# Layer 0's edge types turned in memory, and the softmax stretches of layers 1 and 2 shifted by half a stretch

## The chip, the cores and the metric

The program runs on one core of one Trainium2 chip. Its time is the device time of one execution in microseconds (us). The engines are TensorE (PE), which multiplies matrices, with its weight loads shown as PEld; VectorE (DVE); ScalarE (ACT); GpSimd (POOL), which issues the indirect gathers here; and SyncE (SP), which issues most of the plain transfers. 16 DMA engines carry the transfers.

## The reference

Four graph layers run one after the other over the same graph: 3,125 nodes with 256 features and 50,000 edges, each with a source and a destination. After each layer x becomes layernorm(x + layer(x)). The parts that the change touches, cut to what matters:

```
# layer 0: 16 edge types
e = edge_emb[edge_type]
att_in = concat(x[src], x[dst], e, task)
delta = tanh(gelu(att_in @ att_W1 + b1) @ att_W2 + b2)
w = 1 + edge_scale * delta
agg = segment_sum(messages(x[src], e) * w, dst)
# layer 1: 4 heads, 8 relations; layer 2: 8 heads
score = per edge and head
m = segment_max(score, dst);  ex = exp(score - m[dst])
alpha = ex / segment_sum(ex, dst)[dst]
out = segment_sum(alpha * value[src], dst)
```

Layer 3 is a relational layer with block-diagonal weights; the change does not touch it.

## The kernel before

At the start the edges are sorted by destination and put into 416 *slot tiles* of up to 128 edges. Each slot tile belongs to one of the 25 node tiles of 128 nodes. Four slot tiles make a *group* (104 groups, G = 4) and 16 make a *stretch* (26 stretches, S = 16). The node features stay in SBUF; tables that edges gather from lie in memory.

**Startup.** `bucket` sorts and `segments` (L360) writes, for each slot tile, five rows of marks for the segmented softmax (`seg`): which slots hold an edge and where a node begins and ends. It does so in four chunks of up to 128 slot tiles: matmuls pick each tile's edges (L376, L380), DVE makes the marks (L383 to L400), small matmuls collect the values at tile edges (`astart`, `aend`, `anew`; L402), and an SP transfer stores the chunk. `rows` holds what one tile hands to the next within a stretch.

**Layer 0** walks the groups as a pipeline of three steps, in one loop. `gathered` issues four gathers on POOL (helper at L509) and makes two one-hots of each slot tile on DVE: the place of the edge's destination in its node tile (L928, `places[:, 0]`), and the edge's type (L931), which is copied three times side by side, once for each of three bf16 terms of the type table, into `places[:, 1]` (L934). PE turns both, eight 128x128 transposes a group (L939), and ACT copies the result out of PSUM into `oht` (L943). After every second group SP stores the place one-hots and the turned ones for layers 1 and 2 (`oh_d`, `oht_d`, 256 KB each). `attended` sums the attention's first layer in PSUM (`pre`): the gathered rows with an identity (L956), the destination's part through the turned place one-hot (L961), the type's part through the turned type one-hot and the table `ec` (L964). ACT applies gelu (L965) and DVE multiplies by the second weight and sums along the row (`hg`, L967). `summed` makes the edge weight on ACT (L972, L973), scales the place one-hot by it (`ohw`, L976), and PE sums the messages by destination (`pa`, L979, three PSUM buffers), which DVE adds to `acc` (L981). The two `places` buffers are made once and their unused columns are zeroed at the start (a memset on POOL at L918, another on DVE).

**Layers 1 and 2** share `edge_softmax` (L714). For each stretch it scores the four groups, while it weighs and sums the four groups of the stretch before, and then runs `softmax` (L607), which takes the maximum by destination with scans along the slots of the stretch, hands the state to the next stretch, and gives `ex`. The scores come from a product with the turned one-hots (L1237 in layer 1, L1398 in layer 2; DVE at L1242, L1243 and L1403 to L1405). `weigh` (L682) multiplies the gathered values by `ex` (L697 on DVE, L701 on ACT), sums by destination on PE (L706), and adds to `acc` on DVE (L711). The one-hots come back from memory for eight slot tiles at a time on SP's queue (`onehots_back`, L541), the marks once a stretch (L615, L619). At the beginning of the third stretch of layer 2 (t0 == 2 * S) deferred work, kept in `self.later`, is run.

The program is written in a tile framework: a scheduler fixes the order of the instructions on each engine, and an engine's queue is in order. A buffer of a pool is released as a whole, once everything that reads it is done.

Of the kernel before, what the change touches and what calls it, by code (L numbers as in the profile page):

```python
# [9 lines left out]
F32 = mybir.dt.float32  # L10
BF = mybir.dt.bfloat16
# [7 lines left out]
P = 128  # L19
# [14 lines left out]
class Net:  # L34
# [178 lines left out]
    def bucket(self, src, dst, type16, type8, weight, relations):  # L213
# [12 lines left out]
        self.s_w = c.tile([P, TT], F32, name="s_w")  # L226
        NS = TT // S

# [6 lines left out]

        self.seg = self.dram.tile([TT, 5, P], F32, name="seg")

        self.rows = self.dram.tile([NS, 2, S], F32, name="rows")
        self.astart, self.aend, self.anew = (c.tile([1, TT], F32, name=n) for n in ("astart", "aend", "anew"))
        self.tnode = c.tile([1, TT], I32, name="tnode")  # L240

        with tc.tile_pool(name="bk", bufs=1, side="right") as b:
# [40 lines left out]
            with tc.tile_pool(name="bkw", bufs=1, side="right") as w, tc.tile_pool(name="bkp", bufs=1, space=PSUM) as ps:  # L283
# [73 lines left out]

                self.segments(w, bd, nxt, prv, bdf, sel, kd)

    def segments(self, w, bd, nxt, prv, bdf, sel, kd):  # L360

        tc, nc, TT = self.tc, self.nc, self.TT
        C = bd.shape[1]
        flag = w.tile([P, 2, C, P], F32, name="flag")
# [4 lines left out]
        with tc.tile_pool(name="sgp", bufs=1, space=PSUM) as ps, tc.tile_pool(name="sg", bufs=2, side="right") as v:  # L369
            rows = ps.tile([1, 3, 512], F32, name="rows")  # L370
            for m0 in range(0, TT, P):
# [7 lines left out]
                for k in range(C):  # L379
# [4 lines left out]
                                        op0=ALU.add, op1=ALU.add)  # L384
                nc.vector.tensor_scalar(low[:M], low[:M], float(P), None, op0=ALU.mult)
                sg = v.tile([P, 5, P], F32, name="sg")
                dl = v.tile([P, P], F32, name="dl")
# [13 lines left out]
                for n, col in enumerate((sg[:M, 3, P - 1:P], sg[:M, 4, 0:1], edge[:M])):  # L401
                    nc.tensor.matmul(rows[:, n, m0:m0 + M], col, self.ident[:M, :M], start=True, stop=True)  # L402
                nc.sync.dma_start(self.seg[m0:m0 + M], sg[:M])
            for n, row in enumerate((self.astart, self.aend, self.anew)):
                nc.vector.tensor_copy(row, rows[:, n, :TT])
            rrow = w.tile([1, TT // S, 2, S], F32, name="rrow")
            nc.vector.memset(rrow, NEG)
# [199 lines left out]
    def softmax(self, w, sm, ps, hand, acc, sc, H, F, t0):  # L607
# [4 lines left out]
        nc = self.nc  # L612
        R = H * S
        sg = w.tile([R, 5, P], F32, name="sgm")
        nc.sync.dma_start(sg, bass.AP(tensor=self.seg.tensor, offset=self.seg.offset + t0 * 5 * P,  # L615
                                      ap=[[0, H], [5 * P, S], [1, 5 * P]]))
        s_of = t0 // S
        rr = w.tile([1, 2, H, S], F32, name="rr")
# [33 lines left out]
        nc.vector.scalar_tensor_tensor(hand[(s_of + 1) % 2][:, 0, :, 0], o[:, 0, :, S - 1],  # L652
                                       self.astart[:, t0 + S - 1:t0 + S], outf[:, :, S - 1],
                                       op0=ALU.add, op1=ALU.max)
        if s_of:
            nc.vector.scalar_tensor_tensor(ends[:, 1], o[:, 1, :, 0], self.aend[:, t0:t0 + 1], outb[:, :, 0],
                                           op0=ALU.add, op1=ALU.max)
# [9 lines left out]
        if s_of:  # L667
            dif = sm.tile([1, H], F32, name="dif")
            nc.vector.scalar_tensor_tensor(dif, ends[:, 1], self.anew[:, t0:t0 + 1], o[:, 0, :, 0],
                                           op0=ALU.add, op1=ALU.max)  # L670
            nc.vector.tensor_sub(dif, o[:, 0, :, 0], dif)
            at = sm.tile([1, P], F32, name="at")
            nc.vector.tensor_scalar(at, self.iota[0:1, :], self.s_dl[0:1, t0:t0 + 1], None, op0=ALU.is_equal)
            nc.tensor.matmul(mis[:, 400:400 + H], at, dif, start=True, stop=True)
            fac = sm.tile([P, H], F32, name="fac")
            nc.scalar.activation(fac, mis[:, 400:400 + H], AF.Exp)
            node = self.node_of(nc.vector, t0)
            a3 = acc[:, ds(node * (H * F), H * F)].rearrange("p (h f) -> p h f", h=H)
            self.used(nc.vector, nc.vector.tensor_mul(a3, a3, fac[:, :, None].to_broadcast([P, H, F])))
        yield ex  # L680

    def weigh(self, w, ps, acc, ohb, ex, value, H, t0, on_act):  # L682
# [7 lines left out]
        r = w.tile([P, G, H, F], F32, name="r")  # L690
        s0 = t0 % S
        oh = w.tile([P, G, P], F32, name="oh")
# [21 lines left out]
    def edge_softmax(self, w, sm, ps, hand, acc, H, F, score, on_act):  # L714
# [7 lines left out]
        nc = self.nc  # L722
        before, ex = [], None
        for t0 in range(0, self.TT + S, S):
            last = t0 == self.TT
            if t0 == 2 * S:
                with self.tc.issue_after(self.uses[nc.vector.engine][-1]):
# [3 lines left out]
            if not last:  # L731
                sc = sm.tile([P, H, S], F32, name="sc")
            for n in range(S // G):
                if not last:
                    held.append(score(t0 + n * G, sc[:, :, n * G:(n + 1) * G]))
                if before and (last or n < S // G - 1):
                    value, oh = before[n]
                    done(self.weigh(w, ps, acc, oh, ex, value, H, t0 - S + n * G, on_act))
            if last:
                break  # L740
            rest = iter(())
            if before:
                value, oh = before[-1]
# [10 lines left out]
    def layer0(self, task, edge_emb, msg_W, msg_b, att_W1, att_b1, att_W2, att_b2, edge_scale,  # L754
# [9 lines left out]
        with ExitStack() as layer:  # L764
# [22 lines left out]
            lng = vec(ln_g, D, "lng")  # L787
            lnb = vec(ln_b, D, "lnb")
            ec = wp.tile([P, D], BF, name="ec")
            nc.vector.memset(ec, 0.0)  # L790
            one = wp.tile([P, 1], F32, name="one1")
            nc.vector.memset(one, 1.0)
# [3 lines left out]
            with tc.tile_pool(name="n0", bufs=2) as w, tc.tile_pool(name="m0", bufs=1) as wm, \  # L796
# [20 lines left out]
                ul = film_loads(ua_W1, ua_b1, ua_W2, ua_b2, "ua")  # L817
                E3 = 3 * ET
                emb = wm.tile([E3, D], F32, name="emb")
# [61 lines left out]
                nc.vector.tensor_add(fst[:, 1:2], fst[:, 0:1], fst[:, 2:3])  # L881
                nc.vector.tensor_scalar(fst[:, 1:2], fst[:, 1:2], -1.0, 1.0, op0=ALU.mult, op1=ALU.add)
                nc.vector.tensor_scalar(ecs, part[:, 0, :], fst[:, 0:1], None, op0=ALU.mult)
                for n, o in ((1, ecs), (2, ec[:E3])):
# [26 lines left out]
            with tc.tile_pool(name="e0g", bufs=5) as gp, tc.tile_pool(name="e0", bufs=3) as w, \  # L911
# [3 lines left out]

                places = [hp.tile([P, 2, 2, G, P], BF, name="places%d" % n) for n in range(2)]
                for n, oh in enumerate(places):
                    (nc.vector if n % 2 else nc.gpsimd).memset(oh[:, 1], 0.0)  # L918
                ohts = [None]

                def gathered(t0):
                    gb = gp.tile([P, G, ET + XA], F32, name="gb")
                    for j in range(G):
                        self.gather(gb[:, j, ET:], table, self.s_src, t0 + j)
                    g = t0 // G % 2
                    both = places[t0 // (2 * G) % len(places)]
                    oh = both[:, :, g]
                    nc.vector.tensor_tensor(  # L928
                        oh[:, 0], self.iota[:, None, :].to_broadcast([P, G, P]),
                        self.s_dl[:, t0:t0 + G][:, :, None].to_broadcast([P, G, P]), op=ALU.is_equal)  # L930
                    nc.vector.tensor_tensor(  # L931
                        gb[:, :, 0:ET], self.iota[:, None, :ET].to_broadcast([P, G, ET]),
                        self.s_ty[:, t0:t0 + G][:, :, None].to_broadcast([P, G, ET]), op=ALU.is_equal)
                    nc.vector.tensor_copy(oh[:, 1, :, 0:3 * ET].rearrange("p j (n e) -> p j n e", n=3),  # L934
                                          gb[:, :, None, 0:ET].to_broadcast([P, G, 3, ET]))
                    pt = ps.tile([P, 2, G, P], BF, name="ohp")
                    for n in range(2):
                        for j in range(G):
                            nc.tensor.transpose(pt[:, n, j, :], oh[:, n, j, :], self.idb)  # L939
                    if not g:  # L940
                        ohts[0] = hp.tile([P, 2, 2, G, P], BF, name="oht", bufs=2)
                    oht = ohts[0][:, :, g]
                    nc.scalar.copy(oht, pt)  # L943
                    if g:
                        for to, of in ((self.oh_d, both), (self.oht_d, ohts[0])):
                            nc.sync.dma_start(to[t0 // (2 * G)], of[:, 0].rearrange("p g j v -> p (g j v)"))
                    return t0, gb, oh, oht

                def attended(t0, gb, oh, oht):
                    hg = w.tile([P, G, D], F32, name="hg", bufs=2)  # L950
                    dl = w.tile([P, G], F32, name="dl")
                    for j0 in range(0, G, 2):
# [4 lines left out]
                        for j in (j0, j0 + 1):  # L957
                            q = pre[:, j - j0, :]
                            node = self.node_of(nc.tensor, t0 + j)
                            for n in range(3):  # L960
                                last = nc.tensor.matmul(q, oht[:, 0, j, :], xbr[:, ds(node * (3 * D) + n * D, D)],  # L961
                                                        start=False, stop=False)
                            self.used(nc.tensor, last)
                            nc.tensor.matmul(q, oht[:, 1, j, :], ec, start=False, stop=j > j0)  # L964
                        nc.scalar.activation(hg[:, j0:j0 + 2, :], pre, AF.Gelu)  # L965
# [5 lines left out]
                def summed(t0, gb, oh, dl):  # L971
# [3 lines left out]
                    for j in range(G):  # L975
                        nc.scalar.activation(ohw[:, j, :], oh[:, 0, j, :], AF.Copy, scale=dl[:, j:j + 1])  # L976
                    for j in range(G):
# [658 lines left out]
```

## Time and profile before

| | |
|---|---|
| three runs | 3344.36, 3351.46, 3361.28 us; median 3351.46 |
| the profiled execution | 3366.77 us, of which its span is 3365.0 |
| granted TensorE clock, mean over the span | 0.845 of full speed |
| busy share of the span | PE 80%, DVE 67%, POOL 54%, PEld 52%, ACT 43% |
| startup | to about 215 us |
| layer 0, edges | about 215 to 800 us |
| layer 1, edges | about 1170 to 1812 us |
| layer 2, edges | about 1968 to 2673 us |
| layer 3, edges | about 2830 to 3340 us |

The rest lies in the nodes' work between the layers. A line of the profile's groups reads: line, engine, operation, output from inputs, shape, count, then the busy time in us and the mean of one in ns, then the idle time of that engine just before these instructions and what ended most of it. In a timeline a line has the start, the duration, the engine, the line of code and the operation; several alike in a row are told as one. In the lines of 40 slices each digit is the busy share of a slice of 84 us in tenths.

### The profile page before, as it was taken

The numbers are of one execution on the slowest core, as the hardware profiler recorded it, in microseconds if no ns is written. First come the engines' busy times: TensorE is split into PE (matmuls) and PEld (weight loads), VectorE is DVE, ScalarE is ACT, GpSimd is POOL, SyncE is SP. The second block draws the span as 40 slices with busy tenths as digits, with TensorE's granted clock in tenths as the row PEclk, the third lists the DMA queues.
The fourth block names the chain that finished last, engine by engine and source line by source line (L and its number), as shares of the span: only waits on it lengthen the run. The fifth ranks groups of instructions, "written<-read, shape, count | busy, mean of one in ns | idle before, by whom it ended". The sixth has DMA issues, their size and how long they took to land. (4 is left out here: it accounts for less than half of the span.)

```text
span 3365.0 us, 50575 instructions
## 1 busy us (share of the span) xinstructions
PE 2690.9 (80%) x12679; PEld 1750.5 (52%) x12679; DVE 2267.3 (67%) x6030; ACT 1460.9 (43%) x4405; POOL 1832.7 (54%) x1850
## 2 busy tenths in 40 slices
PE   2779999999979767777775847888888886888885
PEld 1357777775546345555553525666666664333333
DVE  2546676667655479888886437888888873555555
ACT  1427777774456334545543215656656553000001
POOL 3037777771044166666661556766766202777773
PEclk9889999999989878888887968888888886656566
DMA  7249998894067877777774367877877235333333
GB/s 164 74 134 296 298 289 290 288 287 141 32 248 285 313 224 241 231 235 233 231 232 132 123 209 200 227 226 223 228 223 225 78 125 221 106 106 105 105 106 92
DMA packets 240632, 658.40 MB, mean 196 GB/s; under 512 B 47976, under 2 KB 87028, under 8 KB 234029
## 3 DMA queue, kind: packets, MB, share of 16 engines
q0 software_dynamic: 132400, 484.37, 46.9%
q1 hardware_dynamic: 104278, 167.53, 15.2%
q10 hardware_dynamic: 3676, 3.23, 0.5%
q8 instruction: 122, 2.00, 0.2%
q14 instruction: 156, 1.28, 0.1%
HBM read 513.06 MB, written 151.58 MB: 198 GB/s over the span
## 5 line engine op out<-in xcount | busy, mean ns | idle before, releaser
L509 POOL DMA_INDIRECT gb<-table,s_src x832 | 859.1, 1033 | 371.6 <-issue 201.2
L706 PE MATMUL pr<-r,oh 128*128 128x260 f32 x2496 | 735.8, 441 | 82.2 <-DVE acc L711 32.6
L706 PEld LDWEIGHTS pr<-r,oh 128*128 128x128 f32 x2496 | 503.2, 217 | 219.5 <-issue 37.2
L1509 POOL DMA_INDIRECT ring<-table,b_rel x391 | 369.7, 946 | 317.9 <-DVE oh L1519 199.1
L701 ACT ACTIVATE r<-gb,ex 128x64 f32<-128x64 f32 x2080 | 522.3, 335 | 0.0
L509 POOL DMA_INDIRECT gb<-table,s_rel x416 | 404.4, 972 | 205.8 <-issue 110.0
L711 DVE TENSOR_TENSOR acc<-acc,pr 128x260 f32 (+1 forms) x832 | 457.9, 550 | 73.0 <-PE pr L706 59.4
L1538 PE MATMUL pa<-ring,oh 128*128 x832 | 420.5, 617 | 92.3 <-DMA ring<-table,b_rel 44.6
L1538 PEld LDWEIGHTS pa<-ring,oh 128*128 128x128 f32 x832 | 190.7, 278 | 322.4 <-DVE oh L1519 210.8
L1545 DVE TENSOR_TENSOR x<-x,pa 128x256 f32 x416 | 175.2, 421 | 227.8 <-PE pa L1538 225.6
L1237 PE MATMUL pqe<-q_all,oht 128*128 x1248 | 207.1, 304 | 94.6 <-DVE pd L1242 78.7
L693 ACT CAST oh<-ohb 128x512 f32<-128x512 bf16 x208 | 128.3, 618 | 314.2 <-PE pr L706 284.3
L589 ACT ACTIVATE r<-mv,eps 128x4 f32<-128x4 f32 (+2 forms) x31 | 9.1, 295 | 527.8 <-DVE mv L575 524.4
L697 DVE TENSOR_TENSOR r<-gb,ex 128x512 f32<-128x512 f32 (+1 forms) x208 | 225.7, 1086 | 13.3 <-ACT ex L666 9.0
L979 PE MATMUL pa<-gb,ohw 128*128 128x272 f32 x832 | 223.4, 402 | 4.5 <-DVE acc L981 2.9
L1237 PEld LDWEIGHTS <-oht 128*128 128x128 bf16 x1248 | 130.6, 106 | 128.4 <-issue 87.6
L961 PE MATMUL pre<-xb,oht 128*128 x1248 | 193.7, 273 | 0.0
L981 DVE TENSOR_TENSOR acc<-acc,pa 128x272 f32 x416 | 179.7, 432 | 5.1 <-PE pa L979 2.8
L928 DVE TENSOR_TENSOR places<-iota,s_dl 128x512 bf16<-128x512 f32 x104 | 71.9, 691 | 160.8 <-ACT ohw L976 160.8
L956 PE MATMUL pre<-gb,idb 128*128 128x512 bf16 x624 | 169.3, 380 | 5.3 <-DMA gb<-table,s_src 5.3
L967 DVE SCALAR_TENSOR_TENSOR hg<-hg,aw 128x256 f32<-128x256 f32 x416 | 159.3, 420 | 16.4 <-ACT hg L965 16.4
L979 PEld LDWEIGHTS pa<-gb,ohw 128*128 128x128 f32 x832 | 141.2, 190 | 54.6 <-issue 34.0
(383 smaller groups left out, 4302.0 us busy)
## 6 DMA issues: line engine op xcount, KB each, us to landing
ohb<-oh_d SPq DMA_DIRECT2D x104, 256.0 KB
oht<-oht_d SPq DMA_DIRECT2D x104, 256.0 KB
table<-row SPq DMA_DIRECT2D x25, 1024.0 KB
gb<-table,s_src POOLq DMA_INDIRECT x832, 4.5
oh_d<-places SPq DMA_DIRECT2D x52, 256.0 KB
oht_d<-oht SPq DMA_DIRECT2D x52, 256.0 KB
sgm<-seg SPq DMA_DIRECT2D x26, 320.0 KB
gb<-table,s_rel POOLq DMA_INDIRECT x416, 4.7
```

The costliest lines, as they stand in the source:

```text
L509: self.nc.gpsimd.indirect_dma_start(out=out, out_offset=None, in_=table, in_offset=bass.IndirectOffsetOnAxis(ap=idx[:, t:t + 1], axis=0))
L697: nc.vector.tensor_mul(r[:, :, :nd, :hw], v[:, :, :nd, :], ex[:, :nd, s0:s0 + G].rearrange("p h t -> p t h")[:, :, :, None].to_broadcast([ ...
L701: nc.scalar.activation(r[:, j, h, :hw], v[:, j, h, :], AF.Copy, scale=ex[:, h, s0 + j:s0 + j + 1])
L706: nc.tensor.matmul(pr[:, n, :HB * F], oh[:, j, :], r[:, j, n * HB:(n + 1) * HB, :].rearrange("p h f -> p (h f)"), start=True, stop=True)
L711: self.used(nc.vector, nc.vector.tensor_add(a, a, pr[:, :, :HB * F]))
L961: last = nc.tensor.matmul(q, oht[:, 0, j, :], xbr[:, ds(node * (3 * D) + n * D, D)], start=False, stop=False)
L979: nc.tensor.matmul(pa, ohw[:, j, :], gb[:, j, 0:ET + D], start=True, stop=True)
L981: self.used(nc.vector, nc.vector.tensor_add(a, a, pa))
L1237: last = nc.tensor.matmul(pq[:, j, :], oht[:, j, :], q_all[:, ds(node * (3 * D) + n * D, D)], start=n == 0, stop=n == 2)
L1509: st = nc.gpsimd.indirect_dma_start(out=ring[:, at:at + D], out_offset=None, in_=table, in_offset=bass.IndirectOffsetOnAxis(ap=b_rel[:, b: ...
L1538: last = nc.tensor.matmul(pa, oh[:, j, :], ring[:, ds(at, D)], start=True, stop=True)
L1545: self.used(nc.vector, nc.vector.tensor_add(a, a, pa))
```

## The change

In layer 0 the type one-hot is no longer tripled and turned on PE. At startup `segments` also picks each slot tile's edge types with four more matmuls a chunk, copies them to bf16 on ACT, and stores them in memory with one row for a slot tile (`ty_d`). In layer 0 a new function `spread` loads the types of eight slot tiles with one transfer on SP that repeats the same 2 KB on all 128 partitions (256 KB into SBUF, three buffers, 52 transfers), and one DVE comparison a group with a column of numbers (`own`) makes the turned one-hot in place. PE turns only the place one-hots, and ACT's copy is half as wide. `places` and `oht` come from a pool as one tile each for a pair of groups, two buffers of each.

In layers 1 and 2 the marks in memory are padded by half a stretch at either end, and the loop over stretches begins at slot tile -8. So there are 27 stretches, and the first and the last hold eight slot tiles (two groups). The scores of the missing half are set to zero and its marks are neutral.

```diff
 def segments(...)
+                for k in range(C):
+                    nc.tensor.matmul(pk[:M, 3, :], sel[:, k, m0:m0 + M], f16[:, k, :], start=k == 0, stop=k == C - 1)
+                ty = v.tile([P, P], BF, name="ty")
+                nc.scalar.copy(ty[:M], pk[:M, 3, :])
+                nc.sync.dma_start(self.ty_d[m0:m0 + M], ty[:M])
...
-                nc.sync.dma_start(self.seg[m0:m0 + M], sg[:M])
+                M0 = M
+                if m0 + M == TT:
+                    assert M % 32 == 0 and M < P
+                    nc.vector.memset(sg[M:M + L, 0], NEG)
+                    nc.vector.memset(sg[M:M + L, 1:], 0.0)
+                    nc.sync.dma_start(self.seg[0:L], sg[M:M + L])
+                    M0 = M + L
+                nc.sync.dma_start(self.seg[L + m0:L + m0 + M0], sg[:M0])
...
 def edge_softmax(...)
-        before, ex = [], None
-        for t0 in range(0, self.TT + S, S):
-            last = t0 == self.TT
-            if t0 == 2 * S:
+        before, ex, L = [], None, S // 2
+        for t0 in range(-L, self.TT + L + S, S):
+            last = t0 == self.TT + L
+            if t0 == 2 * S - L:
...
                 sc = sm.tile([P, H, S], F32, name="sc")
+                if t0 < 0 or t0 + S > self.TT:
+                    nc.vector.memset(sc, 0.0)
             for n in range(S // G):
+                g0 = t0 + n * G
                 if not last:
-                    held.append(score(t0 + n * G, sc[:, :, n * G:(n + 1) * G]))
-                if before and (last or n < S // G - 1):
+                    held.append(score(g0, sc[:, :, n * G:(n + 1) * G]) if 0 <= g0 < self.TT else None)
+                if before and before[n] and (last or n < S // G - 1):
...
 def layer0(...)
-                places = [hp.tile([P, 2, 2, G, P], BF, name="places%d" % n) for n in range(2)]
-                for n, oh in enumerate(places):
-                    (nc.vector if n % 2 else nc.gpsimd).memset(oh[:, 1], 0.0)
-                ohts = [None]
+                both, types_of = [None], [None]
+
+                def spread(t0):
+                    types_of[0] = t = hp.tile([P, 2, G, P], BF, name="types", bufs=3)
+                    nc.sync.dma_start(t.rearrange("p g j e -> p (g j e)"), bass.AP(
+                        tensor=self.ty_d.tensor, offset=self.ty_d.offset + t0 * P, ap=[[0, P], [1, 2 * G * P]]))
+
+                spread(0)
 
                 def gathered(t0):
...
-                    both = places[t0 // (2 * G) % len(places)]
-                    oh = both[:, :, g]
+                    if not g:
+                        both[0] = [hp.tile([p, 2, G, P], BF, name=n, bufs=2) for p, n in (
+                            (P, "places"), (P, "oht"))] + [types_of[0]]
+                        if t0 + 2 * G < TT:
+                            spread(t0 + 2 * G)
+                    oh, oht, ty = (b[:, g] for b in both[0])
...
-                    nc.vector.tensor_copy(oh[:, 1, :, 0:3 * ET].rearrange("p j (n e) -> p j n e", n=3),
-                                          gb[:, :, None, 0:ET].to_broadcast([P, G, 3, ET]))
-                    pt = ps.tile([P, 2, G, P], BF, name="ohp")
-                    for n in range(2):
-                        for j in range(G):
-                            nc.tensor.transpose(pt[:, n, j, :], oh[:, n, j, :], self.idb)
-                    if not g:
-                        ohts[0] = hp.tile([P, 2, 2, G, P], BF, name="oht", bufs=2)
-                    oht = ohts[0][:, :, g]
+                    pt = ps.tile([P, G, P], BF, name="ohp")
+                    for j in range(G):
+                        nc.tensor.transpose(pt[:, j, :], oh[:, j, :], self.idb)
                     nc.scalar.copy(oht, pt)
...
-                def attended(t0, gb, oh, oht):
+                def attended(t0, gb, oh, oht, ty):
+                    nc.vector.tensor_scalar(ty, ty, own, None, op0=ALU.is_equal)
...
-                            nc.tensor.matmul(q, oht[:, 1, j, :], ec, start=False, stop=j > j0)
+                            nc.tensor.matmul(q, ty[:, j, :], ec, start=False, stop=j > j0)
```

## The prediction

> **What bounds the kernel now.** I read the page's slices first, then the busy time of the engines by stage, because the change touches three stages that have different limits.
>
> ```profile
> PE   2779999999979767777775847888888886888885
> DVE  2546676667655479888886437888888873555555
> PEclk9889999999989878888887968888888886656566
> DMA  7249998894067877777774367877877235333333
> ```
> ```profile
> core 0: us, PE busy (x) PEld busy (x) DVE busy (x) ACT busy (x) POOL busy (x), PEclk, DMA share, GB/s
> 400.00:500.00 100.00, 99.49 (x696) 71.98 (x695) 70.03 (x276) 71.84 (x165) 72.79 (x75) 1.00 0.91 292
> ...
> 1182.00:1211.00 29.00, 16.62 (x83) 10.03 (x82) 18.91 (x24) 1.63 (x3) 18.07 (x19) 0.64 0.76 230
> 1400.00:1500.00 100.00, 76.51 (x401) 53.37 (x399) 88.42 (x183) 50.53 (x196) 65.74 (x69) 0.88 0.75 230
> 2200.00:2300.00 100.00, 83.39 (x370) 62.38 (x369) 85.75 (x189) 61.62 (x242) 68.99 (x64) 0.86 0.80 226
> ```
>
> Layer 0's edges (slices 4 to 9, about 215 to 800 us) keep PE busy 99.5% at full granted clock, with DMA at 0.91 just below. Layers 1 and 2 (1170 to 1812, 1968 to 2673) have no full engine: DVE is at 86 to 88%. The second window is the start of layer 1, where DVE has 10.1 of 29 us free.
>
> Then the timelines of one layer-0 group, which takes 5.42 us (its transposes begin at 504.63, the next group's at 510.05; 104 of them make 564 us):
>
> ```profile
> 502.17 0.69 DVE L928 TENSOR_TENSOR places<-iota,s_dl 128x512 bf16<-128x512 f32 x1 [1.66 <-ACT ohw L976]
> 502.78 0.42 DVE L967 SCALAR_TENSOR_TENSOR hg<-hg,aw 128x256 f32<-128x256 f32 x1
> ...
> 503.51 0.44 DVE L981 TENSOR_TENSOR acc<-acc,pa 128x272 f32 x1
> ```
> ```profile
> 502.65 2.14 PE L979 MATMUL pa<-gb,ohw 128*128 128x272 f32 x8
> 504.63 0.61 PE L939 MATMUL ohp<-idb,places 128*128 128x128 bf16 x8
> 505.07 0.38 PE L956 MATMUL pre<-gb,idb 128*128 128x512 bf16 x1
> ```
> ```profile
> L979 PE MATMUL pa<-gb,ohw 128*128 128x272 f32 x832 | 223.4, 402 | 4.5 <-DVE acc L981 2.9
> L928 DVE TENSOR_TENSOR places<-iota,s_dl 128x512 bf16<-128x512 f32 x104 | 71.9, 691 | 160.8 <-ACT ohw L976 160.8
> ```
>
> The eight transposes cost PE 504.63 to 505.07, 0.44 us. The reader should also see the DVE chain: a new one-hot waits for ACT's last `ohw` that reads the old one, then come two `hg`, then `acc`. There are three `pa` banks for four tiles, so this `acc` (503.51 to 503.95) must free a bank before the fourth product can go (about 504.15). PE lost only 2.9 us to it in all, but it has no slack.
>
> **The change, layer 0.** PE loses four transposes a group: 4 x 55 ns (0.44/8) = 0.22 us, or 0.31 us by the rate of their weight loads (0.62/8). Per pair of groups 0.44 to 0.62 us; alone, over 52 pairs, 23 to 32 us. ACT's copy of 128x1024, 993 ns, becomes 128x512. Its cost lies between the 128x512 gelu on the same engine (588 ns) and nothing saved; near the gelu, so 0.44 saved. That copy stands between the first `ohw` (499.95) and the other three (501.15), so `ohw` ends 0.44 earlier, at 501.70 instead of 502.14. DVE loses the cast (279 ns; 0.17 from start to start) and gains an equality on 128x512 bf16, in place. Before has no such form. Nearest: 128x416 float with one pointer (L312) 431 ns; 128x128 with two pointers (L1519) 341; 128x256 with a constant (L1435) 285. The slope of the last kind gives some 0.5 ns an element, so 0.48 us at 512; ends 0.35 (half the slope) and 0.75 (one element a 1.04 ns cycle added to the same fixed part). Consecutive DVE work overlaps by 0.08, so it takes a spacing s of 0.27 to 0.40, 0.67 at the high end. I take 0.30 to 0.40.
>
> The part that matters is a wait. `places` is now one tile per pair of groups from a pool of two, and pools release a whole tile: the order of instructions has the two one-hots of a pair adjacent on DVE, one wait before both, with the two `hg`, the equality and then `acc` queued behind them. Start at 501.73 (after the earlier `ohw`), two one-hots at 0.61 from start to start: 502.95; two `hg` 0.73: 503.68; s; `acc` 0.44: freed at 504.12 + s; PE goes 0.15 to 0.20 later, about 504.27 + s, against 504.15 less 0 to 0.27 for the transposes already gone. The stall is 0.12 + s to 0.39 + s once a pair: 0.39 to 0.79 us. PE saves 0.44 to 0.62 in the same pair. I take the low half, stall 0.50 and saving 0.55, because the ACT chain is fed by PE's own earlier products and moves forward with it: -0.05 x 52 = -3 us. Ends: all saved, -32; largest stall with smallest saving, +0.35 x 52 = +18.
>
> DMA gains 52 loads of 256 KB on SP: 128 packets of 2 KB each. One-hot stores of 2 KB took 84 ns a packet, the startup's bias rows spread to 128 partitions 116 mean. On 16 engines that is 0.67 to 0.93 us a pair, onto 0.903 x 10.85 = 9.80: 10.5 to 10.7, a floor of 5.24 to 5.37 us a group. It lies beside PE and is not the end, but leaves 1 to 3%. The load has been issued two pairs ahead of its use, some 10 to 15 us, behind the two stores on SP.
>
> The Trainium skill, "SBUF — State Buffer", section "Who interferes with whom", says that a `tensor_scalar` can take the port pair that VectorE shares with GpSimd and then fully blocks GpSimd's descriptor writing. In layer 3 416 such DVE instructions ran beside GpSimd's 391 gathers: 337 to 547 ns, median 341, and the gathers kept 946. By the rule layer 0 would be worse: four gathers with issue, 4 x 1.25 = 5.0, plus 0.48, estimated 5.48 a group and +6 us; by the row nothing. I count nothing.
>
> **Startup.** Four chunks each add four matmuls (eight passes of 0.12 = 0.97 us) on PE, where it waits 1.97 to 2.39 us for DVE's `sg` (L394, L396); ACT's copies are in an idle engine; SP gets four stores and a load more before the first products (224.2, which wait for a gather). Zeroing of `places` (POOL 0.95, DVE 0.48) goes. -1 to +4; I take 0. If PE's cover were gone it would be +3.9.
>
> **Layers 1 and 2.** The shift adds a 27th softmax a layer. On DVE, L627 to L679 in the rows of 1784 to 1795: 0.27 + 2 x 0.41 + 0.21 + 0.27 + 0.25 + 0.21 + 0.20 + 2 x 0.33 + 0.28 + 0.20 + 0.14 + 0.27 + 0.42 = 4.2 us; layer 2 with 0.70 for the last term and longer scans 4.9. In return weighing can begin after two groups, not four. Layer 1: two groups' weighing on DVE, 2 x (0.69 + 4 x 0.42) = 4.7. With the softmax that is 8.9, and the start has 10.1 free, so between -4.7 (all hidden) and +4.2. At its end 28 us (1783 to 1811) hold 6.4 idle, of which the long softmax waits (0.42 + 2.01 + 0.42 and ends) are about 4, which the earlier stretch's weighing may fill: 0 to -4. I take -2 and -2: -4, ends -9 and +4.
>
> Layer 2's start is different: PE waits for a transposed one-hot tile.
>
> ```profile
> 2009.18 0.55 PE L1398 MATMUL pst<-s_tgt,oht 128*128 x4 [14.74 <-DMA oht<-oht_d]
> 2010.42 0.58 PE L633 MATMUL mis<-ident,smf 128*1 128x128 f32 x2 [0.68 <-DVE smf L629]
> ```
>
> SP's queue has 2.6 MB of `x` ahead of the third load. In the new order the same two loads precede `x`, and PE's first softmax part that combines the scans stands behind the two score products of the third, so the first `ex` still comes after 2009; it was 2016.0, and loses only the 4 to 6 us of second-half softmax. The end (21.8 us to weigh four groups, against 25 a steady stretch) only redistributes. So -6 to +5 (the extra softmax not hidden), I take -1.
>
> Sum: -3 + 0 - 4 - 1 = -8 us. The profiled execution took 3366.77 us (span 3365.0 and 1.77 outside), 15.3 above the median 3351.46, so the same kernel would profile at about 3359, and its median is 3343.
>
> **The rivals.** A (faster): the paired wait doesn't bite, since ACT frees the one-hots earlier still or DVE slips `acc` ahead. For it: DVE idles 1.66 us before every `places`. Against: the in-order queue just described. Layer 0 then goes -18 to -32 (DMA's upper floor of 5.37 would keep 5); total about -27, 3324. B (slower): the same wait with s at 0.67. It decides where 0.12 to 0.39 + s exceeds 0.55, s about 0.16 to 0.43; at 0.67 the stall is 0.79 to 1.06, at least +0.24 x 52 = +12 to +27; with layers 1 and 2 at -5 the total is +14, 3365. C: the extra softmaxes are paid in full and nothing comes back, +9, with layer 0 at -3: 3357. D: DMA nears full use and the types come late; once a pair up to 1 us, +52 at worst, usually +5: 3356.
>
> **How the numbers follow.** Forecast 0.42, A 0.25, B 0.18, C 0.10, D 0.05. A change below 0.5%, 16.8 us, can't be told from none: faster is below 3334.7, slower above 3368.2. The forecast by its ends runs 3326 to 3358; a fifth of it counts as faster. Nearly all of A is faster; half of B and a sixth of C and D are slower, to which I add a little for several mishaps together. Faster 0.33, same 0.48, slower 0.19. The range 3314 to 3372 reaches into A's and B's bounds.
>
> **What would show it.** Layer 0's group at 5.36 to 5.42 us, PE waits on `acc` once a pair (tens of us instead of 2.9): the stall. Group at 5.2 and PE at 99%: A. DMA above 0.96 with PE waiting on types: D. The equality's mean duration decides B. First `r` of layer 1 at about 1200 to 1204 less the shift of what precedes, instead of 1211.5; first `ex` of layer 2 still after the third `oht` load. I am wrong if DVE's order differs on the chip from the queue (it can't reorder), if the pair wait is hidden by ACT, or if the cost of broadcast packets from one 2 KB of memory is several times 116 ns.

## The result and the profile after

The changed kernel takes 3453.77 us (median of four runs, 3450.56 to 3457.81) against 3356.19 before (four runs beside it): a ratio of 1.0284, 95% interval 1.0263 to 1.0305. It is 2.8% slower, where the forecast was 0.2% faster (3343 us, with a range of 3314 to 3372).

The profiled execution took 3452.89 us with a span of 3451.1, so 86.1 us more span than the one shown of before. The medians differ by 97.6: the profiled execution of before was 10.6 above its median, that of after 0.9 below. The 86.1 can be split at four instructions that both kernels have. In us, from the starts of the first and last records of these lines, each to about 0.1:

| | start to first `pre` | layer 0, first `pre` to last `pa` | to layer 2's first score | layer 2, first score to last `pr` | rest |
|---|---|---|---|---|---|
| before | 224.2 | 574.2 | 1176.5 | 696.8 | 693.3 |
| after | 226.7 | 648.3 | 1175.3 | 706.5 | 694.3 |
| difference | +2.5 | **+74.1** | -1.2 | **+9.7** | +1.0 |

The slices and the windows of after, which answer to the lines shown of before (columns as there):

```profile
PE   2878888888979967777775766888888787988885
DVE  2546666666665548888888455888888873555556
DMA  8148888888127877777775356777888425333333
```
```profile
400.00:500.00 100.00, 85.84 (x557) 61.09 (x555) 64.29 (x243) 55.24 (x146) 61.62 (x65) 1.00 0.84 274
600.00:700.00 100.00, 85.55 (x538) 60.08 (x537) 62.80 (x239) 52.91 (x139) 59.81 (x62) 0.98 0.84 271
```

In layer 0 PE is busy 86%, not 99.5%, at a granted clock of 1.00 and 0.98. Every other engine is less busy too, and DMA moves less in a second than before. Nothing is full any more, so the time went into waiting. The costliest groups of the page say for whom PE waits; the line's own query says what DVE waits for (in the second fence: total us and number of waits):

```profile
L1007 PE MATMUL pa<-gb,ohw 128*128 128x272 f32 x832 | 227.4, 402 | 86.4 <-DVE acc L1009 85.5
L1009 DVE TENSOR_TENSOR acc<-acc,pa 128x272 f32 x416 | 180.5, 434 | 15.2 <-PE pa L1007 12.7
```
```profile
L977 DVE TENSOR_SCALAR types<-types,own x104: 334/353/595, 220.3 to 844.4; 128x512 bf16<-128x512 bf16 x104
its engine sat idle before it (us, times) until:
  DMA types<-ty_d: 125.2, 51
```

PE's wait on `acc` grew from 2.9 us to 85.5. DVE stands 125.2 us, 2.45 us once in each of 51 pairs of groups, before the new equality, until a load of types lands. Now the timelines of one pair, SP first, then DVE, then PE:

```profile
499.81 0.32 SPq L945 DMA_DIRECT2D types<-ty_d  x1
502.66 0.32 SPq L973 DMA_DIRECT2D oht_d<-oht  x1
507.05 0.32 SPq L973 DMA_DIRECT2D oh_d<-places  x1
```
```profile
505.12 0.35 DVE L977 TENSOR_SCALAR types<-types,own 128x512 bf16<-128x512 bf16 x1 [2.88 <-DMA types<-ty_d]
505.39 0.43 DVE L1009 TENSOR_TENSOR acc<-acc,pa 128x272 f32 x1
505.74 1.29 DVE L961 TENSOR_TENSOR places<-iota,s_dl 128x512 bf16<-128x512 f32 x2
...
507.63 0.35 DVE L977 TENSOR_SCALAR types<-types,own 128x512 bf16<-128x512 bf16 x1
507.89 0.43 DVE L1009 TENSOR_TENSOR acc<-acc,pa 128x272 f32 x1
```
```profile
505.96 0.70 PE L1007 MATMUL pa<-gb,ohw 128*128 128x272 f32 x2 [0.16 <-DVE acc L1009]
508.47 0.94 PE L1007 MATMUL pa<-gb,ohw 128*128 128x272 f32 x2 [1.81 <-DVE acc L1009]
```

The load goes out at 499.81 and DVE can compare at 505.12. The `acc` behind it and the two one-hots all come later, and PE's next product stands 1.81 us. But the products that use this very comparison come only much later. Counted over the middle of the layer, a load is issued about 27.6 us before the first product that uses it, and the equality starts 4.9 us after the issue. That is 22.9 us (first group of a pair) and 28.0 us (second) before its use. The load is early enough for PE. It is DVE's queue that takes the equality about two pairs too soon, and so meets the load that was just sent.

Why the load goes out when it does, is told by SP's own waits in the window of 300 to 700 us (total, times, longest):

```profile
SPq L945 <- PE pre L992: 168.8, 32, 6.7
```

There are three buffers, the equality is made in place, and so a buffer is free only when PE's last product with those types is done.

### The profile page after: what moved, and what is told of

The parts are those of the page before. It is cut to its first block, busy times and chain, and to the rows that moved or that the text cites. A ratio compares the mean times of both kernels' runs of the same rounds, so it can differ in the third digit from the quotient of the medians.

```text
span 3451.1 us, 50049 instructions
## 1 busy us (share of the span) xinstructions
PE 2704.1 (78%) x12319; PEld 1749.8 (51%) x12319; DVE 2292.7 (66%) x6071; ACT 1409.3 (41%) x4417; POOL 1818.2 (53%) x1849
## 3 DMA queue, kind: packets, MB, share of 16 engines
q8 instruction: 119, 1.95, 0.2%
## 5 line engine op out<-in xcount | busy, mean ns | idle before, releaser
L525 POOL DMA_INDIRECT gb<-table,s_src x832 | 845.9, 1017 | 602.5 <-issue 204.5
L1007 PE MATMUL pa<-gb,ohw 128*128 128x272 f32 x832 | 227.4, 402 | 86.4 <-DVE acc L1009 85.5
L1265 PEld LDWEIGHTS <-oht 128*128 128x128 bf16 x1248 | 129.1, 105 | 119.0 <-issue 77.5
L989 PEld LDWEIGHTS <-oht 128*128 128x128 bf16 x1248 | 124.6, 100 | 63.2 <-issue 5.2
```

The lines of the kernel that those rows point to most:

```text
L525: self.nc.gpsimd.indirect_dma_start(out=out, out_offset=None, in_=table, in_offset=bass.IndirectOffsetOnAxis(ap=idx[:, t:t + 1], axis=0))
L989: last = nc.tensor.matmul(q, oht[:, j, :], xbr[:, ds(node * (3 * D) + n * D, D)], start=False, stop=False)
L1007: nc.tensor.matmul(pa, ohw[:, j, :], gb[:, j, 0:ET + D], start=True, stop=True)
L1265: last = nc.tensor.matmul(pq[:, j, :], oht[:, j, :], q_all[:, ds(node * (3 * D) + n * D, D)], start=n == 0, stop=n == 2)
```

## The experiments

**Which of the two edits.** e1_stretches has only the shift in layers 1 and 2, e2_types only the types from memory in layer 0. Both are taken whole from the change.

> Only the shifted stretches of layers 1 and 2, layer 0 as before. If the loss is layer 0's alone, the time is 3351 to 3358 us as before. From the traces of both kernels I rather expect the layers' own share to stay: layer 1 about -1, layer 2 about +10, so some +9 us, about 3365 us (ratio 1.003).

> Only layer 0's types from memory, stretches as before. Theory (the equality on DVE waits for the types' load, 125 us of DVE waits in 51 pairs): layer 0 keeps its +74 us, so about 3430 us (ratio 1.022), with DVE waiting about 125 us on the load. Rival (the two edits cost together, through what layer 0 leaves for the later layers): clearly less than +60.

Measured: the shift alone has ratio 1.0020 (1.0004 to 1.0037), the types alone 1.0224 (1.0177 to 1.0271). With the four instructions as above: e1 spends 573.4 us in layer 0 (before 574.2), 1175.7 to layer 2's first score, and 706.8 in layer 2. e2 spends 647.0 in layer 0 and 693.4 in layer 2, and DVE waits 125.8 us on the types. So the edits add up stage by stage, and each of these two stages' difference belongs to one edit.

**Is the load late, or the comparison early?** e6_held leaves loads, buffers and arithmetic, and only holds the equality back in DVE's order, until the accumulation of three groups earlier:

```diff
-                    nc.vector.tensor_scalar(ty, ty, own, None, op0=ALU.is_equal)
+                    with self.tc.issue_after(self.uses[nc.vector.engine][-5:][0]) if t0 >= 4 * G else ExitStack():
+                        nc.vector.tensor_scalar(ty, ty, own, None, op0=ALU.is_equal)
```

> The changed kernel with the equality held back in DVE's order until the accumulation of three groups earlier, the same loads and buffers. Theory (DVE takes the equality about 25 us ahead of the product that uses it, and so meets a load that was issued only 5 us before): DVE's wait for the load falls from 125 us to below 10, layer 0 from 648 us to 560 to 580, the time to about 3365 us (3350 to 3385). Rival 1 (the 256 KB broadcast load itself is slow or overloads DMA): it is late here as well and the time stays above 3420. Rival 2 (the paired wait of the place one-hots that the prediction feared): PE's wait on the accumulation stays at some tens of us.

e4_types6 gives the types six buffers instead of three.

```diff
-                    types_of[0] = t = hp.tile([P, 2, G, P], BF, name="types", bufs=3)
+                    types_of[0] = t = hp.tile([P, 2, G, P], BF, name="types", bufs=6)
```

> The changed kernel with six instead of three buffers for the types. If only buffers are short, loads go out three pairs earlier, the wait goes and the time is about 3365 us. By my theory the order on DVE moves the equality ahead by as many pairs as there are buffers, so that it still meets a load just issued: DVE waits 100 to 125 us for it and the time stays at 3435 to 3455 us.

Measured: e6 has ratio 0.9987 (0.9968 to 1.0005), 3359.74 us. Windows, and the equality's waits, of e6:

```profile
400.00:500.00 100.00, 99.46 (x651) 71.87 (x650) 76.00 (x285) 65.26 (x174) 76.64 (x77) 1.00 0.94 325
600.00:700.00 100.00, 99.44 (x649) 71.70 (x648) 75.90 (x284) 65.26 (x174) 76.81 (x77) 1.00 0.94 324
```
```profile
L978 DVE TENSOR_SCALAR types<-types,own x104: 346/348/585, 227.7 to 772.5; 128x512 bf16<-128x512 bf16 x104
its engine sat idle before it (us, times) until:
  DMA types<-ty_d: 0.7, 1
```

DVE's wait is 0.7 us, PE is full again, and layer 0 takes 550.5 us: 97.8 less than the changed kernel with the same loads, and 23.7 less than before. The equality now runs 18.8 us after its load's issue and 5.1 to 5.4 us before its use. e4 has ratio 1.0253 (1.0214 to 1.0292), DVE waits 116.2 us and layer 0 takes 643.8. Its equality runs 60.6 to 65.1 us ahead of its use and still 5.0 us after the issue: the order on DVE moved it forward with the buffers. So the comparison is early, and more buffers don't help.

**What remains of the stall that the prediction feared.** e5_separate writes the equality to a tile of its own, so that a loaded tile is free as soon as DVE has compared it. e3_oneload has the same place for the equality, but leaves the repeated loads out: the first eight slot tiles' types serve for all.

```diff
-                    nc.vector.tensor_scalar(ty, ty, own, None, op0=ALU.is_equal)
+                    raw = ty
+                    ty = w.tile([P, G, P], BF, name="turned", bufs=3)
+                    nc.vector.tensor_scalar(ty, raw, own, None, op0=ALU.is_equal)
```

and in e3 alone:

```diff
-                        if t0 + 2 * G < TT:
-                            spread(t0 + 2 * G)
```

> The changed kernel with the equality written to a tile of its own (three buffers of one group), so that the loaded types are free as soon as DVE has compared them. Theory (a load goes out only when PE has used the tile two pairs before, because the equality is in place): loads go out earlier, DVE's wait on them is below 10 us, layer 0 from first to last product 545 to 565 us, total about 3360. Rival (the broadcast load takes long however early it is issued): DVE still waits over 50 us.

> The changed kernel without the repeated loads: the types of the first eight slot tiles are loaded once and compared again for every group, into a tile of their own, so layer 0's output is not the reference's; the equality stands ahead of the accumulation as in e5. If the broadcast loads cost something of themselves (DMA share, late landing), layer 0 from first to last product falls clearly below e5's 574 us, to 550; if what is left in e5 is only the place of the equality in DVE's order, it stays at 568 to 576.

Measured: e5 3383.98 us, one run beside 3363.25 before. DVE's wait for loads is 0.9 us in all, as the theory said, but layer 0 takes 573.7 us, not 545 to 565. The reason is in e5's waits (300 to 780 us) and in DVE's order:

```profile
PE pa L1009 <- DVE acc L1011: 17.2, 45, 0.4
```
```profile
507.73 1.29 DVE L961 TENSOR_TENSOR places<-iota,s_dl 128x512 bf16<-128x512 f32 x2 [1.13 <-ACT ohw L1006]
508.94 0.42 DVE L997 SCALAR_TENSOR_TENSOR hg<-hg,aw 128x256 f32<-128x256 f32 x1
509.28 0.42 DVE L997 SCALAR_TENSOR_TENSOR hg<-hg,aw 128x256 f32<-128x256 f32 x1
509.63 0.35 DVE L979 TENSOR_SCALAR turned<-types,own 128x512 bf16<-128x512 bf16 x1
509.89 0.43 DVE L1011 TENSOR_TENSOR acc<-acc,pa 128x272 f32 x1
```

This is the chain of the prediction, one-hot, one-hot, `hg`, `hg`, equality, `acc`, and it eats the whole gain of the transposes: 573.7 against 550.5 of e6, (573.7 - 550.5) / 52 = 0.45 us a pair. In e6 the same two one-hots stand together, and only the equality has left the place ahead of that `acc`. e3 without the loads takes 573.1 us in layer 0 (3383.75 us in all, one run): the 13.6 MB of broadcasts cost no time that shows where the order on DVE sets the pace. Where PE sets it, in e6, no kernel without the loads was run, but PE is 99.4% busy with them.

**The startup, and the parts that pay.** e7_types_held is e6 without the shift. e8_transposed also makes the types for memory elsewhere: four transposes of the slot tiles' type columns, in `bucket`, in place of the 32 matmuls between the marks.

```diff
-                for k in range(C):
-                    nc.tensor.matmul(pk[:M, 3, :], sel[:, k, m0:m0 + M], f16[:, k, :], start=k == 0, stop=k == C - 1)
...
                 nc.scalar.copy(self.s_ty, p)
+                p = ps.tile([P, C, P], F32, name="ptt", tag="pick", bufs=3)
+                for m0 in range(0, TT, P):
+                    M = min(P, TT - m0)
+                    nc.tensor.transpose(p[:M, m0 // P, :], self.s_ty[:, m0:m0 + M], self.ident)
...
```

e9_layer1_only is e8 with the stretches of layer 1 shifted and those of layer 2 not (with the marks padded, and a second `rows` for the unshifted stretches):

```diff
-        before, ex, L = [], None, S // 2
+        before, ex, L = [], None, S // 2 if H == 4 else 0
+        self.shift = L
```

> Layer 0's types from memory with the equality held back, stretches as before. If the two edits add up (e6_held at ratio 0.9987, the stretches alone at 1.002), the ratio is 0.9967, some 11 us below before: layer 0's groups -24 us, the startup +10. Rival: the held equality's gain came from the shifted stretches too, then the ratio is at 0.9987 or above.

> As e7, but the types for memory are turned from the slot tiles' own type columns by four transposes, outside the loop over the four chunks of marks. Theory (the four matmuls, the copy by ScalarE and DVE's wait for that copy stand in one chain in each chunk, 2.5 us a chunk, so the startup grew by 10 us): the startup falls by 7 to 10 us, ratio 0.9938 to 0.9947. Rival (they lay under PE's old wait for the marks, as predicted, and the startup varies by itself): no difference from e7, within 2 us.

> As e8, with the stretches of layer 1 shifted and those of layer 2 as before. From the traces layer 1 gains 1 to 4 us by the shift and layer 2 loses 10: so 0 to 4 us below e8 and layer 2 from its first score to its last sum back at 697 us. Rival (layer 2's loss comes from the padded marks or from what layer 1 leaves): layer 2 stays at 707.

Measured, on one chip: e7 0.9952 (0.9938 to 0.9966), e8 0.9941 (0.9923 to 0.9960), e9 0.9948 (0.9930 to 0.9965). e7 was expected at 0.9967, just above its interval; its layer 0 takes 550.9 us and its layer 2 695.1, so the two edits add up here too. From the first matmul with `flag` to the last that fills `rows` there pass 26.7 us in before, 37.2 in after, 37.1 in e2, 37.2 in e7, and 26.8 in e8. The first `pre` starts at 232.4 in e7 and 225.3 in e8. That is the expected 7 to 10 us, although the medians (3348.19, 3341.39) overlap in their intervals. DVE's and ACT's timelines of after show the chain in one chunk:

```profile
189.93 0.15 DVE L388 TENSOR_SCALAR low<-low 128x1 f32<-128x1 f32 x1
191.44 0.35 DVE L396 TENSOR_SCALAR dl<-pk,low 128x128 f32<-128x128 f32 x1 [1.36 <-ACT ty L392]
```
```profile
191.14 0.27 ACT L392 CAST ty<-pk 128x128 bf16<-128x128 f32 x1 [10.48 <-PE pk L390]
```

The types' matmuls write over the column that `low` reads, in the same PSUM tile, so they start after `low`; and `dl`, which reads another part of that tile, waits for ACT's copy.

The chain is only about half of the 10.5 us. The windows of this stretch in before, after and e1 (columns as before):

```profile
184.47:211.40 26.93, 18.25 (x147) 15.71 (x145) 11.38 (x50) 0.00 (x0) 0.00 (x0) 0.92 0.10 38
176.15:213.50 37.35, 27.61 (x179) 23.55 (x177) 12.04 (x52) 1.05 (x4) 0.00 (x0) 0.77 0.09 31
184.07:215.23 31.16, 22.43 (x147) 19.18 (x145) 11.99 (x52) 0.00 (x0) 0.00 (x0) 0.78 0.09 34
```

In after the types' matmuls hold PE for 4.5 us, and PE waits 1.1 us for `low` before them. The other 4.8 us lie in matmuls that before has too: the granted clock was 0.77, against 0.92 in before, and the 16 products with `flag` of the third chunk took 3.28 us where those of the first took 1.95. e1 has no types' matmuls, but a granted clock of 0.78, and takes 31.0 us. e8 and e9 have 0.94. What lowers the clock there is not shown, so the gain of e8 over e7 is that of the chain and of the clock (0.77 in e7) together.

In e9 layer 2 is back at 695.0 us (with the shift 706.5 in after, 706.8 in e1 and e6), and from layer 0's end to layer 2's first score it takes 1176.4 us, e8 1176.5. The shift costs layer 2 about 10: apart from the two runs on another chip, which follow below, it takes 705 to 708 us in every run that shifts it and 692 to 697 in every run that does not. Layer 1's edges alone, from the first `pqe` product to the last `pr`, are 1.0 to 2.4 us shorter with the shift in each of four pairs of profiles (before and e1, e2 and after, e7 and e6, e8 and e9). In three of the pairs 1.4 to 1.6 us of this are lost again by layer 2's first score, and what is left, 0.1 to 1.7 us, can't be told from none.

**Layer 2's ten microseconds.** e10_back_act is e8 with the loads of x issued on ACT's queue instead of SP's (all but the last partial tile; five transfers, 3.1 MB by the trace, not the 2.6 of the prediction); e11_shift_back_act is the same with both layers shifted.

```diff
-                    self.back(self.x.rearrange("p t d -> p (t d)"), own[:, :D])
+                    self.back(self.x.rearrange("p t d -> p (t d)"), own[:, :D], nc.scalar)
```

> As e8 (stretches unshifted), with the 2.6 MB of x that layer 2 loads back issued on ScalarE's queue rather than on SP's, where they stand before the third load of turned one-hots (PE waits 14.7 us for that load). If the queue is what holds the first scores, layer 2's first exponentials come 5 to 12 us earlier and the time falls to a ratio of 0.991 to 0.993. Rival (the transfers share the DMA engines with the gathers anyway, or ScalarE is held up): the same as e8, ratio 0.994, or above.

> As e10, but with the stretches of layers 1 and 2 shifted. If the late load of one-hots is what keeps the shift from paying in layer 2, layer 2 from first score to last sum falls from 707 to about e10's value and the ratio is that of e10 or below. Rival (the half stretch at the end and the empty gather queue at the start cost the 10 us): some 10 us above e10.

These two ran on a chip on which the kernel before took 4050.18 us at a granted clock of 0.81 to 0.82, and in e10 PE was busy 79 to 84% of layer 0's windows, so they are compared only with each other there: e10 0.9892 (0.9838 to 0.9946), e11 0.9931 (0.9890 to 0.9973), and layer 2 803.4 and 812.4 us. With x off SP's queue the shift still costs layer 2 nine. e12_back_act is e10 again:

> The kernel of e10 once more, since the run of e10 fell on a chip on which the kernel before took 4050 us. If SP's queue holds layer 2's first scores, layer 2 from first score to last sum is 685 to 690 us (e8: 692) and the ratio 0.990 to 0.993; if not, as e8, 0.994.

It has ratio 0.9936 (0.9921 to 0.9950) and layer 2 at 693.6 us, as e8 (692.3): the first exponentials come 39.2 us after the first score instead of 41.4, and layer 2 is not shorter for it. Where the shift loses is seen in windows between consecutive exponentials, in e1 and then in before:

```profile
2015.50:2034.90 19.40, 13.33 (x58) 9.96 (x57) 12.29 (x32) 8.03 (x31) 8.10 (x8) 0.72 0.64 171
2034.90:2067.70 32.80, 22.84 (x88) 16.46 (x88) 21.12 (x43) 15.44 (x60) 16.30 (x16) 0.84 0.57 167
...
2646.70:2671.70 25.00, 20.63 (x80) 15.44 (x80) 20.27 (x41) 15.28 (x60) 0.00 (x0) 0.86 0.00 0
2671.70:2684.00 12.30, 9.25 (x34) 7.43 (x34) 8.56 (x11) 6.52 (x28) 0.00 (x0) 0.86 0.32 75
```
```profile
2016.00:2044.70 28.70, 20.84 (x86) 15.00 (x85) 20.14 (x39) 15.32 (x59) 16.45 (x16) 0.82 0.71 189
2044.70:2071.80 27.10, 20.88 (x84) 15.78 (x84) 21.16 (x45) 15.39 (x60) 16.78 (x16) 0.85 0.69 196
...
2651.20:2673.00 21.80, 17.62 (x66) 14.03 (x66) 17.39 (x22) 13.74 (x56) 0.00 (x0) 0.85 0.16 39
```

In e1 the first exponentials come only 2.3 us sooner after the first score (38.8 against 41.1). The next full stretch then takes 32.8 us, in which GpSimd stands 9.0 us before a gather until DVE frees a buffer (`r`). The last stretch scores two groups and still takes the full 25.0. The saving after the last exponentials is 8.8 us (20.5 to 11.7, to the start of the last `pr`). Between the first and the last exponentials lie 26 intervals of 25.2 us in the mean instead of 25 of 25.4, which is 656.2 us against 635.2. So one more stretch costs 21.0 us, and start and end give 11.1 back, which leaves 9.9. That the shift in layer 2 is the cause is shown by e1 and e9; the split between start and end is read from the traces and was not tried apart.

The best versions, e8 and e12, are about 0.6% faster than before; they can't be told apart.

## Why the prediction was wrong

**The step that failed** is the sentence on the load: "The load has been issued two pairs ahead of its use, some 10 to 15 us, behind the two stores on SP." The lead over the product's use was even longer, 27.6 us (two pairs at the prediction's own 10.85 us would be 21.7, not 10 to 15). But the first user of the load is the equality, and between issue and equality lie 4.9 us. The prediction counted the equality's place on DVE only as 0.27 to 0.67 us ahead of `acc`, and not as a wait for a transfer on an in-order engine. By e5, which has everything but that wait, it cost 648.3 - 573.7 = 74.6 us. Rival D named late types, with "usually +5" and at worst +52, but as the effect of DMA near full use. DMA's share was 0.84, so D came true in its sign and not in its cause.

**The chain of the paired one-hots** was right, and hidden by the load's wait: e5 and e3, which have the chain without the wait, take 573.7 and 573.1 us in layer 0 against 574.2. That is -0.5 and -1.1 where the sum said -3. The stall was 0.45 us a pair against the 0.50 taken, and the saving 0.46 (23.7 / 52) against 0.55.

**The transposes** were priced rightly: with neither wait (e6, e7, e8) layer 0 gains 22.8 to 23.7 us, at the low end of the 23 to 32. Rival A's premise, PE at 99% with a pair of groups in 10.5 us (5.25 a group), occurs only there.

**The equality** took 353 ns median, so s was near 0.27; rival B's 0.67 was not met. DMA was no bound: e6 ran at a share of 0.94 and 325 GB/s, where 0.97 to 0.99 had been worked out. The gathers' packets of 5 KB took 260 ns in the mean in before and 235 in e6 (300 to 700 us), so a floor added up from before's share did not hold. The Trainium skill's rule ("SBUF — State Buffer", "Who interferes with whom") that such an instruction can block GpSimd's descriptor writing does not show here: the gathers' median was 946 ns in before and in after and 947 in e6, and PE was full in e6.

**The startup** was taken at 0 and costs some 10 us (37.2 against 26.7). The prediction laid the matmuls under PE's wait for the marks, but the wait is behind them in the same chain: PE still waits about 2.08 us there, after the new work. The bound that it gave for no cover, +3.9, was also too small: the matmuls held PE for 4.5 us, PE's wait for `low` (1.1) was left out, and the old matmuls ran 4.8 us longer at a lower granted clock, which stays open. In the profile of after only 2.5 us show, as its marks began 5 to 9 us earlier (176.1; 181.3 to 184.9 in the other runs, and 178.4 on the slower chip); why is open.

**Layer 1** was taken at -4 and gave 0.1 to 1.7; **layer 2** at -1, with +5 as its upper end, and lost 9.7. The late first exponentials were foreseen. What failed was "only redistributes" for the end: a stretch with half the scores takes as long as a full one (25.0 us in e1).

## What to carry to other kernels

A load is late or early for the first instruction in a queue that touches it, not for the one that needs the value. When work with much slack (a comparison, a conversion) is added to an in-order engine, look where the scheduler puts it, and count the time from the load's issue to that place; a scheduler that moves it forward as far as buffers allow makes more buffers useless, and holding it back cost nothing here. A shorter first stage pays only if the stage behind it can start with what it then has.

## What was not expected of the hardware

A 256 KB load that repeats the same 2 KB on 128 partitions was ready for DVE about 4.9 us after its issue with DMA at a share of 0.84, and 52 of them had no price in a stage at a DMA share of 0.90 (e3, without them, 573.1 us in layer 0) and 0.94 to 0.95 (e5, with them, 573.7). And the same kernel before took 3344 to 3380 us on the other chips and 4050 (median; granted clock 0.81 to 0.82) on one, with layer 0 of the types' version (e10) at 746 us from first to last product and PE at 79 to 84%. Why that chip is slower is not shown. Within one startup the same 16 products took 1.95 and 3.28 us, with a granted clock of 0.77 over the stretch.
